# An adaptive-norm block with a gated scan and an FP4 feed-forward: loads, maxima and the last store moved to other places

## The chip, the core and the metric

The kernel runs on one NeuronCore of a Trainium2 chip. Its engines are named as in the profile: PE (matrix multiply; PEld is its weight load), DVE (vector), ACT (scalar activation), POOL (general purpose) and SP, which here only issues DMAs. Each engine works through its own instructions in program order and waits for others by semaphores. The metric is the device time of one execution in microseconds (us), as the median of several runs; one further execution was taken with the hardware profiler.

## The reference, cut to what matters

```python
mod = (silu(c) @ wmod).reshape(B, 6, 1, -1)        # sa, ca, ga, sb, cb, gb; B = 2
h = layernorm(x) * (1 + ca) + sa                    # x: 2 x 4096 x 512, fp32
xn = h / norm(h) * d**0.5 * gamma
q, kv, a = split(einsum('bnd,ed->bne', xn, W_qkva), 3)
y = scan over n of  y = sigmoid(a) * y + kv
x = x + ga * (q * y)
h = layernorm(x) * (1 + cb) + sb
gate, up = fp4_linear(h, w_gate), fp4_linear(h, w_up)   # 512 -> 1408
x = x + gb * fp4_linear(silu(gate) * up, w_down)        # 1408 -> 512
```

`fp4_linear` rounds both operands to a 4-bit grid in blocks of 16, each block scaled by its largest absolute value, before the product. ga and gb are kept at least 0.25 away from zero.

## The kernel before, in words

Every product is made from 16-bit halves: a factor is split into a high and a low part ("hl") and three of the four products are summed, 36 matmuls for one 128-row part of q, kv and a over 512 tokens. A tile of tokens is 128 rows; there are 64 (NT). A DMA transpose issued by SP brings each hl into the layout that PE needs.

*Part one* (`start()` and the loop at L766) makes norm, projection, scan and residual. A block is 512 tokens, 16 blocks in all (NBLK). A **slot** is one block and one quarter e of the 512 features, so 64 slots (NS); three more drain the pipeline. In slot s PE makes a, kv and q of that quarter (`mix`, L384) into three of six PSUM banks, which alternate between even and odd slots. One slot later ACT makes the sigmoid (`gates`, L405), DVE the scan (L411) and the product with q (L420), ACT splits y into 16-bit halves (L427), and SP transposes them; two slots later ACT joins the halves (L435) and POOL adds them to x and stores the rows to `out` (L443, L445). Beside it the norm of the tiles of the next block runs: `norm_load`, `norm_moments`, `norm_stats` (POOL, L160 and L161), `norm_center` (L166), `norm_shift` (L172), `norm_square` (ACT, L354), `norm_gain` (POOL, L359 and L361), `norm_hi` (ACT, L367), `norm_lo` (DVE, L372) and the transpose into xT (L376). The tile for which slot s issues its xT is s + 4, so the last xT of a block is issued in the slot before PE starts on it.

The projection's weights come in four groups e of three 128 x 512 parts: `load_qkva`, `gamma_qkva` (times gamma, L281, on POOL or DVE), `square_qkva` (ACT, L285), `inverse_qkva` and `gain_qkva` (POOL powers, L289 and L299; `scale_qkva` calls both), `hi_qkva` and `lo_qkva` (L310, L316) with a transpose into wqT (L324). Groups 0 to 2 are prepared in `start()`, group 3 in slots 0 and 1.

The weights of the feed-forward are prepared in the background, by a written-out plan of **units**, one step of the plan a slot: slots 6 to 16 take block maxima of the gate and up weights, slots 17 to 22 those of the down weights (`weight_max`), then `spread_max` sends the maxima of the 128 partitions through DRAM (L483, L484) and a slot later `finish_max` reduces them (L489); from then on each slot rounds one tile of weights (`quant_rows`, `quant_down`). A unit's load is issued one slot before its work. `Unit.advance` interleaves its steps with the norm's.

Near the end of part one, slot 58 (NS - 6) loads three modulation rows for part two, each spread over 128 partitions (L267), and four tiles of x from `out` (`load_x1`, L575).

*Part two* (the loop at L957) goes over the 64 tiles of tokens: `products` (gate and up, L871), `silu`, `gated`, `quant_h`, and two tiles later `down` (L918) and `finish`, which multiplies by gb and adds to `out` with an accumulating DMA of POOL (L941). `quant_x` prepares the tile two ahead.

The order on every engine is the order of the program text (`manual_schedule`). SP's DMAs count on eight semaphores in turn, so each also waits until the eighth before it has landed. The tiles "ld" are a ring of six, "hl" of four, "o" of three.

Of the kernel before, what the change touches and what calls it, by code (L numbers as in the profile page):

```python
# [17 lines left out]
P = 128  # L18
D = 512
# [24 lines left out]
def tile_adaln_block(  # L44
# [173 lines left out]
    def mod_spread(s, b):  # L218
        pm = side((P, D))
        for k in range(KC):  # L220
            T.matmul(
                pm,
                sc[:, k, b : b + 1].to_broadcast([P, P]),
                wm[s][:, k, :],
                start=k == 0,
                stop=k == KC - 1,
            )
        return pm
# [47 lines left out]
    def load_qkva(e):  # L276
        for part in (2, 1, 0):
            load_part(e, part)
# [51 lines left out]
    def norm_load(g):  # L330
        i, t = divmod(g, KC)
        if i not in xrows:
            xrows[i] = apool.tile([P, KC, D], F32, name="xr", tag="xr", bufs=4)
        xld[g] = xrows[i][:, t, :]
        b, t0 = divmod(g * P, N)
        S.dma_start(xld[g], x[b, t0 : t0 + P, :])
# [130 lines left out]
    def weight_max(wt, am, col, first):  # L467
        block_max(am, wt)
        V.tensor_scalar(am, am, 6e-12, TIE / 6.0, ALU.max, ALU.mult)
        if first:  # L470
            V.tensor_reduce(gsum[:, col : col + 1], am, AX.X, ALU.max)
        else:
            m = small.tile([P, 1], F32, name="gm", tag="gm")
            V.tensor_reduce(m, am, AX.X, ALU.max)
            V.tensor_tensor(gsum[:, col : col + 1], gsum[:, col : col + 1], m, ALU.max)
# [2 lines left out]

    peaks = []

    def spread_max():
        gall = apool.tile([P, P, 3], F32, name="gall", tag="row", bufs=1)
        G.dma_start(gmax, gsum)  # L483
        G.dma_start(gall, gmax.unsqueeze(0).to_broadcast([P, P, 3]))  # L484
        peaks.append(gall)

# [50 lines left out]
    downs = [(i, j) for i in range(KC) for j, _ in WIDE]  # L537
    for n in range(0, len(downs), 2):
        plan.append([("maxd", r) for r in downs[n : n + 2]])
    plan.append([("spread", None)])  # L540
    plan.append([("finish", None)])
    for n, r in enumerate(rows):
# [68 lines left out]
    class Unit:  # L611
# [9 lines left out]
        def advance(self, pos):  # L621
            if self.kind in ("rows", "down"):
                if pos == self.step:
                    next(self.gen, None)
                    self.step += 1
            elif pos == 3:
                if self.kind == "max":
                    i, col, _, ams = self.arg
                    weight_max(self.wt, ams[i], col, i == 0)
                elif self.kind == "maxd":  # L630
                    i, j = self.arg
                    weight_max(self.wt, am_d[i][j], 2, self.arg == (0, 0))
                elif self.kind == "spread":
                    spread_max()
                else:
                    finish_max()
                self.step = 7
# [4 lines left out]
    def start():  # L642
        a, b_, c_ = PARTS

        def load_mod_piece(s, k):
            S.dma_start(wm[s][:, k, :], wmod[k * P : (k + 1) * P, s * D : (s + 1) * D])

        load_mod(1, KC)
        norm_load(0)
        S.dma_start(gam, gamma.partition_broadcast(P))  # L650
        for k, then in enumerate((PARTS[0], PARTS[1], PARTS[2], None)):
            if then is None:
                norm_load(1)
            else:
                load_part(0, then)
            load_mod_piece(0, k)
        norm_load(2)
        norm_load(3)
        pc = mod_spread(1, 0)
        ps = mod_spread(0, 0)  # L660
        r1 = mod_rows(1)
        r0 = mod_rows(0)

        norm_moments(0)
        norm_stats(0)
        gamma_qkva(0, a, V)
        A.activation(ca[0], pc, AF.Copy, bias=1.0)
        square_qkva(0, a)
        gamma_qkva(0, b_, V)
        square_qkva(0, b_)  # L670
        inverse_qkva(0, a, a + 1)
        norm_center(0)
        gamma_qkva(0, c_, V)
        inverse_qkva(0, b_, b_ + 1)
        hi_qkva(0, a, True)
        square_qkva(0, c_)
        lo_qkva(0, a)
        inverse_qkva(0, c_, c_ + 1)
        hi_qkva(0, b_, True)
        norm_moments(1)  # L680
        norm_stats(1)
        lo_qkva(0, b_)
        A.copy(sa[0], ps)
        norm_center(1)
        hi_qkva(0, c_, True)
        norm_shift(0)
        norm_square(0)
        lo_qkva(0, c_)
        load_qkva(1)
        norm_gain(0, G)  # L690
        norm_shift(1)
        norm_square(1)
        norm_hi(0)
        norm_moments(2)
        norm_moments(3)
        norm_gain(1, G)
        norm_stats(2)
        norm_hi(1)
        norm_stats(3)
        norm_lo(0, xT)  # L700
        load_mod(2)
        norm_center(2)
        norm_shift(2)
        norm_square(2)
        norm_lo(1, xT)
        load_qkva(2)
        norm_gain(2, G)
        norm_center(3)
        norm_shift(3)
        norm_square(3)  # L710
        norm_gain(3, G)
        norm_hi(2)
        gamma_qkva(1, a, V)
        norm_lo(2, xT)
        norm_load(KC)
        norm_hi(3)
        gamma_qkva(1, b_, V)
        square_qkva(1, a)
        square_qkva(1, b_)
        norm_lo(3, xT)  # L720
        norm_load(KC + 1)
        inverse_qkva(1, b_, a + 1)
        gamma_qkva(1, c_, V)
        mod_store(*r1, tag="yh")
        square_qkva(1, c_)
        mod_store(*r0)
        hi_qkva(1, a, False)
        inverse_qkva(1, c_, c_ + 1)
        for part in PARTS:
            gamma_qkva(2, part)  # L730
        lo_qkva(1, a)
        hi_qkva(1, b_, True)
        norm_moments(KC)
        hi_qkva(1, c_, True)
        lo_qkva(1, b_)
        norm_stats(KC)
        lo_qkva(1, c_)
        norm_load(KC + 2)
        load_qkva(3)
        norm_center(KC)  # L740
        for part in PARTS:
            square_qkva(2, part)
        norm_shift(KC)
        norm_square(KC)
        norm_gain(KC, G)
        gain_qkva(0)
        norm_moments(KC + 1)
        inverse_qkva(2)
        norm_stats(KC + 1)
        for part in PARTS:  # L750
            hi_qkva(2, part, False)
            lo_qkva(2, part)
        gain_qkva(1)
        gain_qkva(2)
# [8 lines left out]
    with order:  # L763
        xT = new_xT()
        start()
        for slot in range(NS + 3):  # L766
# [19 lines left out]
                residual(*joined(*joining.pop(0)))  # L786
            if g < NT:
                norm_hi(g)
            if slot == 0:
                for part in PARTS:  # L790
                    gamma_qkva(3, part)
                    square_qkva(3, part)
            if gate is not None:
                gate = scan(*gate)
            if slot == 1:
# [9 lines left out]
                joining.append(halves(*gate))  # L805
            if slot == 1:
                for part in PARTS:
                    hi_qkva(3, part, False)
                    lo_qkva(3, part)
            if g + 2 < NT:  # L810
                norm_stats(g + 2)
            for u in units:
# [6 lines left out]
            if g + 1 < NT:  # L819
                norm_shift(g + 1)  # L820
                norm_square(g + 1)
            for u in units:
                u.advance(4)
            coming = [Unit(*c_) for c_ in coming]
# [1 line left out]
                u.advance(0)  # L826
            if g + 1 < NT:
                norm_gain(g + 1, G)
            for u in units:
                u.advance(5)  # L830
                u.advance(6)
            assert all(u.step == 7 for u in units)
            if slot == 0:
                scale_qkva(3)
            if 0 < slot < KC:
                prep_gain(slot)
            if slot + 2 in MODS:
# [3 lines left out]
            if slot == KC + 1:  # L841
                ca[1] = mod_load(1, 1, "mod_c1")
                sa[1] = mod_load(0, 1, "mod_s1")
            if slot == NS - 6:
                mods_for(0)
                gbs[0] = mod_load(5, 0, "mod_gb")
                x1s = {n: load_x1(n) for n in range(4)}
            if NS - 5 <= slot < NS - 1:
                n = slot - NS + 5
                xst[n] = stats_x(x1s[n])  # L850
# [77 lines left out]
    def finish(i, pd, u):  # L928
        b, t0 = divmod(i * P, N)
        if b not in gbs:  # L930
            t = ring.tile([P, D], F32, name="mod_gb1", tag="mod_gb1", bufs=1)
            S.dma_start(t, modd[5][b : b + 1, :].to_broadcast([P, D]))
            gbs[b] = t
        o = ring.tile([P, D], F32, name="o", tag="o", bufs=3)
        parts = 2 if i == NT - 1 else 1
        for d0 in range(0, D, D // parts):
            d = slice(d0, d0 + D // parts)
            V.scalar_tensor_tensor(  # L938
                out=o[:, d], in0=pd[:, d], scalar=u, in1=gbs[b][:, d], op0=ALU.mult, op1=ALU.mult
            )  # L940
            G.dma_start(out[b, t0 : t0 + P, d], o[:, d], accum_op=ALU.add)  # L941

    LAG, LEAD = 2, 2
    qh = {}
# [9 lines left out]
    with tc.manual_schedule(engines={V.engine, A.engine, G.engine, S.engine, T.engine}):  # L954
        h = None
        ended = []
        for i in range(NT):  # L957
# [27 lines left out]
            h = quant_h(i, work_i[2])  # L985
            step(h, 3)
        step(h, 2)
        finish(*ended.pop(0))
        step(h, 3)
        ended.append(down(NT - 2))  # L990
# [45 lines left out]
```

## Time and profile before

| | |
|---|---|
| median of 3 runs | 1947.03 us (1947.01 to 1948.91) |
| profiled execution | 1951.17 us |
| its span | 1949.0 us |
| mean granted clock of PE | 0.992 |
| PE busy | 1912.0 us, 98% |
| DVE busy | 1601.0 us, 82% |
| ACT busy | 991.2 us, 51% |
| POOL busy | 423.2 us, 22% |
| PE's first matmul | at 4.94 us |
| PE's first matmul of part two | at 572.5 us |
| PE's last matmul ends | at about 1942.3 us |

All times in views of the trace are us from the start of the span. A line of the timeline gives start, duration, engine, source line, operation, output and input, count, and in brackets how long the engine stood idle before and what released it. The releaser is inferred from the semaphores, and where several were waited for it is the last by the profile. The row of an issuing DMA (SPq, or POOL with DMA_DIRECT2D) is the time of the issue, not of the transfer. A window row gives its length, the busy time of PE, PEld, DVE, ACT and POOL, then the clock that was granted to PE (1.00 is full speed), the busy share of the DMA engines and GB/s.

### The profile page before, as it was taken

Reading aid. Unit: us, or ns where it says so; the run is one execution under the profiler, and the core shown is the slowest. Engines: PE = TensorE matmul, PEld = TensorE weight load, DVE = VectorE, ACT = ScalarE, POOL = GpSimd, SP = SyncE. Lnnn points to the kernel's source line nnn. Section 1 sums busy time; section 2 is a strip of 40 time slices with the busy share of each in tenths; the row PEclk is TensorE's granted clock in tenths of the full one; section 3 lists DMA queues with packets and bytes.
Section 4 is the critical chain, followed back from the end, with each engine's and each line's share of the span. In section 5 each row is a group of like instructions: output and inputs, shape, how many; then the busy total and the mean of one; then the engine's idle time right before and its main releaser. Section 6 shows DMA issues by size and latency. Waiting matters only on the chain.

```text
span 1949.0 us, 25684 instructions
## 1 busy us (share of the span) xinstructions
PE 1912.0 (98%) x9220; PEld 901.3 (46%) x9220; DVE 1601.0 (82%) x2669; ACT 991.2 (51%) x1705; POOL 423.2 (22%) x605
## 2 busy tenths in 40 slices
PE   7799999999999999999999999999999999999998
PEld 4344434444444444444444444444444444444443
DVE  5677889999859988888888888888888888888864
ACT  4444467777655544444444444544454454444432
POOL 4544456666530100000000000001001000000000
PEclk9899999999999999999999999999999999999999
DMA  9688689999843443533443344334434433433333
GB/s 235 145 238 199 171 169 200 202 203 200 187 103 63 78 78 63 82 74 63 73 80 67 63 79 88 63 68 88 69 63 78 79 63 64 82 73 63 68 62 51
DMA packets 483007, 206.39 MB, mean 106 GB/s; under 512 B 439558, under 2 KB 440838, under 8 KB 482880
## 3 DMA queue, kind: packets, MB, share of 16 engines
q1 hardware_dynamic: 468144, 170.98, 41.9%
q0 software_dynamic: 14736, 33.78, 10.6%
q8 instruction: 72, 1.18, 0.3%
q14 instruction: 55, 0.45, 0.1%
HBM read 62.85 MB, written 33.58 MB: 49 GB/s over the span
## 4 chain that ended last, share of the span: by engine, by line
PE 79%; issue 5%; DVE 1%; DMA 1%; POOL 0%; SPq 0%; ACT 0%; POOLq 0%; ACTq 0%; DVEq 0%
PE mm L871 44%; PE sd L918 21%; PE mm L393 14%; DMA xT<-hl 1%; POOL out_dram L941 0%; DVE ld L172 0%; DVE y L420 0%; DVE hl L372 0%; DVE ld L166 0%; SPq L575 0%; DVE xn L106 0%; DVE st L153 0%; SPq L267 0%; SPq L529 0%; DVE hl L129 0%
## 5 line engine op out<-in xcount | busy, mean ns | idle before, releaser
L871 PEld LDWEIGHTS <-x2T 128*128 128x128 f16 x4608 | 450.8, 98 | 469.4 <-issue 1.2
L393 PE MATMUL mm<-xT,wqT 128*128 128x512 f16 (+1 forms) x2412 | 511.5, 376 | 23.9 <-DMA xT<-hl 17.0
L871 PE MATMUL mm<-wuT,x2T 128*128 128x512 f16 (+1 forms) x2304 | 487.7, 361 | 1.0 <-DVE hid L891 1.0
L871 PE MATMUL mm<-wgT,x2T 128*128 128x512 f16 (+1 forms) x2304 | 487.7, 361 | 0.0
L918 PE MATMUL sd<-wdT,hT 128*128 128x512 f16 x2112 | 465.8, 379 | 0.0
L393 PEld LDWEIGHTS <-wqT 128*128 128x128 f16 x2412 | 233.5, 99 | 303.3 <-issue 37.7
L918 PEld LDWEIGHTS <-hT 128*128 128x128 f16 x2112 | 206.7, 98 | 242.6
L886 ACT ACTIVATE silu<-mm,u 128x512 f32<-128x512 f32 (+1 forms) x192 | 124.7, 650 | 285.3 <-PE mm L871 281.4
L891 DVE SCALAR_TENSOR_TENSOR hid<-mm,u,silu 128x512 f32<-128x512 f32 (+1 forms) x192 | 128.5, 673 | 140.0 <-PE mm L871 131.0
L587 POOL TENSOR_SCALAR rstd<-vs 128x1 f32<-128x1 f32 x64 | 15.2, 238 | 986.2 <-ACT sq L585 986.2
L143 ACT ACTIVATE u<-ud,rms 128x1 f32<-128x1 f32 x64 | 18.9, 295 | 278.2 <-DVE rms L139 278.2
L120 ACT ACTIVATE sle<-sl 128x512 f16<-128x512 f32 (+2 forms) x162 | 146.9, 907 | 0.0
L113 ACT ACTIVATE she<-sh 128x1408 bf16<-128x1408 bf16 (+1 forms) x128 | 128.3, 1003 | 4.0
L941 POOL DMA_DIRECT2D out_dram<-o x65 | 58.0, 898 | 275.7 <-DVE o L938 271.9
L411 DVE TENSOR_TENSOR_SCAN y<-sig,cy,mm 128x512 f32<-128x512 f32 x56 | 71.6, 1279 | 52.2 <-ACT sig L405 22.2
L427 ACT COPY yh<-y 128x1024 uint16<-128x1024 uint16 x64 | 66.9, 1046 | 79.8 <-DVE y L420 75.6
L122 DVE SCALAR_TENSOR_TENSOR xn<-hid,xn 128x1408 f32<-128x1408 f32 x64 | 103.6, 1618 | 3.7 <-ACT hid L116 3.7
L106 DVE TENSOR_TENSOR xn<-hid,inv 128x1408 f32<-128x1408 f32 x64 | 104.0, 1625 | 2.2
L125 DVE SCALAR_TENSOR_TENSOR hhl<-hid,xn 128x1408 f16<-128x1408 f32 x64 | 104.0, 1625 | 2.2
L147 DVE TENSOR_REDUCE amh<-hid 128x88 f32<-128x1408 f32 x64 | 103.7, 1620 | 2.2
L116 ACT ACTIVATE hid<-xn 128x1408 f32<-128x1408 f32 x64 | 88.2, 1378 | 30.9 <-DVE xn L106 30.9
L443 POOL TENSOR_TENSOR xr<-xr,y 128x512 f32<-128x512 f32 x64 | 81.4, 1273 | 56.4 <-ACT y L435 54.4
(113 smaller groups left out, 1913.0 us busy)
## 6 DMA issues: line engine op xcount, KB each, us to landing
xr<-in_L_attn_x_dram SPq DMA_DIRECT2D x64, 256.0 KB, 3.5
out_dram<-xr POOLq DMA_DIRECT2D x64, 256.0 KB, 4.0
ld<-out_dram SPq DMA_DIRECT2D x64, 256.0 KB, 2.9
out_dram<-o POOLq DMA_DIRECT2D x63, 256.0 KB, 4.1
ld<-in_L_ffn_w_gate_dram SPq DMA_DIRECT2D x22, 256.0 KB, 3.4
ld<-in_L_ffn_w_up_dram SPq DMA_DIRECT2D x22, 256.0 KB, 3.4
scratch<-in_L_wmod_dram SPq DMA_DIRECT2D x4, 1024.0 KB, 5.7
ld<-in_L_ffn_w_down_dram SPq DMA_DIRECT2D x16, 256.0 KB, 3.4
```

Source lines behind the costliest of these rows:

```text
L106: V.tensor_tensor(blocks(xn), blocks(src), spread(inv, nb), ALU.mult)
L113: A.activation(blocks(she), spread(sh, nb), AF.Copy, scale=WPEAK)
L116: A.activation(a, xn, AF.Abs, scale=MAGIC)
L120: A.activation(blocks(sle), spread(sl, nb), AF.Copy, scale=WPEAK)
L122: V.scalar_tensor_tensor(out=xn, in0=a, scalar=FLOOR, in1=xn, op0=ALU.max, op1=ALU.add)
L125: V.scalar_tensor_tensor(out=nq, in0=a, scalar=FLOOR, in1=xn, op0=ALU.max, op1=ALU.subtract)
L147: V.tensor_reduce(am, src.rearrange("p (b k) -> p b k", k=QB), AX.X, ALU.max, apply_absolute_value=True)
L393: T.matmul(pp[:, t : t + width], wqT[:, wp * KC + k, r * P : (r + 1) * P], xT[:, xp * KC + k, t : t + width], start=n == 0, stop=n == 3 * ...
L871: T.matmul(pp[:, : n1 - n0], x2T[:, xp * KC + k, :], wt[:, wp * KC + k, n0:n1], start=n == 0, stop=n == 3 * KC - 1,)
L886: A.activation(sl[:, :w], pairs[j][0][:, :w], AF.Silu, scale=u[:, 0:1])
L891: V.scalar_tensor_tensor(out=hid[:, n0:n1], in0=pairs[j][1][:, : n1 - n0], scalar=u[:, 1:2], in1=sl[:, : n1 - n0], op0=ALU.mult, op1=ALU.mult,
L918: T.matmul(pd, hT[:, hp * IC + k, :], wdT[:, wd_chunk(wp, k), :], start=n == 0, stop=n == 3 * IC - 1,)
```

## The change

- In `start()` the loads of the second weight group and of the first tile of block 1 go out before the first transposes; the 1 MB load of wmod (`load_mod(2)`) goes behind the second tile's xT, and the loads of the third weight group behind the fourth.
- The fourth weight group: its products with gamma (POOL) move to the end of slot 0, behind the norm's gain; its squares (ACT) from slot 0 to slot 1, behind the halves of y; scales, high and low parts (POOL, DVE) to the end of slot 1, behind the norm's shift and square.
- The maxima take three slots: `collect_max` issues the store in one, `spread_max` the load in the next, `finish_max` follows in the third. All later units move by one slot.
- At the end of part one the modulation rows are loaded in slots 36 and 38, and two tiles of x each in slots 58 and 59.
- The last tile of tokens isn't added to `out` by the DMA: DVE adds x, loaded by SP beforehand, and SP stores the sum in two halves.

```diff
+    def collect_max():
+        G.dma_start(gmax, gsum)
+
     def spread_max():
         gall = apool.tile([P, P, 3], F32, name="gall", tag="row", bufs=1)
-        G.dma_start(gmax, gsum)
         G.dma_start(gall, gmax.unsqueeze(0).to_broadcast([P, P, 3]))
...
+    plan.append([("collect", None)])
     plan.append([("spread", None)])
     plan.append([("finish", None)])
...
         norm_load(2)
         norm_load(3)
+        load_qkva(1)
+        norm_load(KC)
         pc = mod_spread(1, 0)
...
         lo_qkva(0, c_)
-        load_qkva(1)
         norm_gain(0, G)
...
         norm_lo(0, xT)
-        load_mod(2)
         norm_center(2)
         norm_shift(2)
         norm_square(2)
         norm_lo(1, xT)
-        load_qkva(2)
+        load_mod(2)
         norm_gain(2, G)
...
         norm_lo(2, xT)
-        norm_load(KC)
         norm_hi(3)
...
         norm_lo(3, xT)
+        load_qkva(2)
         norm_load(KC + 1)
...
             if g < NT:
                 norm_hi(g)
-            if slot == 0:
-                for part in PARTS:
-                    gamma_qkva(3, part)
-                    square_qkva(3, part)
...
             if slot == 1:
                 for part in PARTS:
-                    hi_qkva(3, part, False)
-                    lo_qkva(3, part)
+                    square_qkva(3, part)
...
                 norm_shift(g + 1)
                 norm_square(g + 1)
+            if slot == 1:
+                scale_qkva(3)
+                for part in PARTS:
+                    hi_qkva(3, part, False)
+                    lo_qkva(3, part)
...
             if g + 1 < NT:
                 norm_gain(g + 1, G)
+            if slot == 0:
+                for part in PARTS:
+                    gamma_qkva(3, part)
...
-            if slot == 0:
-                scale_qkva(3)
...
-            if slot == NS - 6:
+            if slot == NS // 2 + KC:
                 mods_for(0)
+            if slot == NS // 2 + KC + 2:
                 gbs[0] = mod_load(5, 0, "mod_gb")
-                x1s = {n: load_x1(n) for n in range(4)}
+            if slot in (NS - 6, NS - 5):
+                for n in range(2):
+                    n += 2 * (slot - NS + 6)
+                    x1s[n] = load_x1(n)
...
-        parts = 2 if i == NT - 1 else 1
-        for d0 in range(0, D, D // parts):
-            d = slice(d0, d0 + D // parts)
+        def scaled(d):
             V.scalar_tensor_tensor(
                 out=o[:, d], in0=pd[:, d], scalar=u, in1=gbs[b][:, d], op0=ALU.mult, op1=ALU.mult
             )
-            G.dma_start(out[b, t0 : t0 + P, d], o[:, d], accum_op=ALU.add)
+
+        if i < NT - 1:
+            scaled(slice(0, D))
+            G.dma_start(out[b, t0 : t0 + P, :], o, accum_op=ALU.add)
+            return
+        for d0 in range(0, D, D // 2):
+            d = slice(d0, d0 + D // 2)
+            scaled(d)
+            V.tensor_tensor(o[:, d], o[:, d], last_x1[:, d], ALU.add)
+            S.dma_start(out[b, t0 : t0 + P, d], o[:, d])
...
         step(h, 2)
+        last_x1 = load_x1(NT - 1)
         finish(*ended.pop(0))
```

More of the change, by code (lines that the diff above doesn't have):

```diff
@@ L632, in advance @@
                     weight_max(self.wt, am_d[i][j], 2, self.arg == (0, 0))
+                elif self.kind == "collect":
+                    collect_max()
                 elif self.kind == "spread":
```

## The prediction, made blind

> **What bounds the kernel now.** I read the waits of PE first, then PE alone in order of time, then the engines around each gap, then the granted clock in windows of 2 us. PE is busy 98% of the span, so only its idle time and the time at a lowered clock can be won. Its waits, as engine, line, what was waited for, total us, times, longest:
>
> ```profile
> PE mm L393 <- DMA xT<-hl: 17.0, 6, 5.7
> PE mm L393 <- ACT sig L405: 6.9, 2, 4.7
> PE sd L221 <- DMA scratch<-in_L_wmod_dram: 5.4, 3, 4.9
> PE mm L871 <- DVE hid L891: 1.0, 1, 1.0
> ```
>
> Nearly all of it is part one (L393). In order of time (start, duration, count, and in brackets the idle time before):
>
> ```profile
> 26.23 2.17 PE L393 MATMUL mm<-xT,wqT 128*128 128x128 f16 x36 [2.65 <-DMA xT<-hl]
> 31.88 5.54 PE L393 MATMUL mm<-xT,wqT 128*128 128x128 f16 x72 [3.48 <-DMA xT<-hl]
> ...
> 56.30 18.72 PE L393 MATMUL mm<-xT,wqT 128*128 128x512 f16 x72 [4.69 <-ACT sig L405]
> 80.75 41.58 PE L393 MATMUL mm<-xT,wqT 128*128 128x512 f16 x180 [5.72 <-DMA xT<-hl]
> ...
> 251.95 32.93 PE L393 MATMUL mm<-xT,wqT 128*128 128x512 f16 x144 [2.18 <-ACT sig L405]
> 286.90 243.36 PE L393 MATMUL mm<-xT,wqT 128*128 128x512 f16 x1119 [2.02 <-DMA xT<-hl]
> ```
>
> A slot is 36 such matmuls at 216 ns, 7.78 us. Counting them, the gaps lie inside slot 0 (26, 32), before slot 2 (56.30), slot 4 (80.75), slot 24 (251.95), slot 28 (286.90) and slot 60 (539.76, 2.38 us, also xT). Between slots 4 and 24 PE has no gap. After a gap PE also runs slowly for a while: 144 matmuls in 32.93 us instead of 31.1. The windows around slot 24 show why (the seventh figure is the clock, behind the five engines):
>
> ```profile
> 252.00:254.00 2.00, 2.00 (x8) 0.84 (x9) 0.95 (x2) 0.04 (x1) 0.00 (x0) 0.80 1.14 221
> 254.00:256.00 2.00, 2.00 (x6) 0.76 (x5) 0.00 (x0) 0.00 (x0) 0.44 (x1) 0.50 0.54 47
> 256.00:258.00 2.00, 2.00 (x10) 0.79 (x8) 0.05 (x1) 0.80 (x2) 1.84 (x4) 0.84 0.73 82
> ```
>
> 2 us x (0.20 + 0.50 + 0.16) = 1.7 us lost on top of a gap of 2.18.
>
> **A rule that would shrink the gain.** The Trainium skill ("TensorE: Matmul & The Clock Gate", section "Why this matters for your kernels") asks for no idle gaps over about 3 us between bursts, since one idle window brings the half clock. By it, gaps of 2.0 to 2.4 us cost only themselves. The rows disagree: the three gaps at slots 24, 28 and 60 are all shorter, and each is followed by the half clock (slot 28: 1.6 us lost in the windows 286 to 292; slot 60: 144 matmuls in 32.93 us, 1.8 lost). I take the rows. By the rule my sum would be 3.4 us smaller.
>
> **Maxima over three slots (slot 28).** POOL and what hung on it, in slots 23 and 24:
>
> ```profile
> 250.00 0.64 POOL L483 DMA_DIRECT2D gmax<-gsum  x1
> 255.56 0.56 POOL L484 DMA_DIRECT2D gall<-gmax  x1 [4.92 <-DMA gmax<-gsum]
> ...
> 257.12 0.72 ACT L367 ACTIVATE hl<-ld,rn 128x512 f16<-128x512 f32 x1 [5.07 <-POOL rn L361]
> ```
>
> POOL stands 4.92 us for the first DMA; behind it on POOL are L359 and L361, which ACT's L367 needs, and behind that DVE (5.00 us). The scans run 251.08, 263.34, then every 7.56: one slot of 12.3. So xT for slot 28 was issued at 281.70 and landed about 286.7, while PE was ready at 284.88. With the second DMA a slot later nothing is queued behind a wait: the first DMA (5.3 us from issue to landing) is down before POOL gets there, and the second (3.9) before DVE reads gall another slot on. Gain 2.02 + 1.6 = 3.6. The gap before slot 24 stays: xT of slot 23 was issued at 248.15, before all this, because the maxima slots take the other engines 8.35 us (scans 228.21, 236.56, 244.91) against PE's 7.78. It moves with the start. All weight work runs a slot later, at 7.56 us of DVE a slot against 7.78, and its last unit falls in slot 59, where DVE has no norm work left (it idled 7.15 us there): 0.
>
> **Loads off the end of part one (slot 60).** SP's queue before the last xT:
>
> ```profile
> 528.39 1.52 SPq L267 DMA_DIRECT2D mod<-modd  x3
> ...
> 529.96 1.92 SPq L575 DMA_DIRECT2D ld<-out_dram  x4
> 531.99 3.38 SPq L376 DMA_TRANSPOSE xT<-hl  x1
> ```
>
> Seven loads of 256 KB stand ahead of it; it takes about 7.6 us to land (539.6), against 4.9 median in slots 43 to 59. PE was ready at 537.39. Afterwards two loads stand ahead. The two that go to slot 59 are issued behind it; three go to slots 36 and 38. Issue at 531.2 (its data is ready at 531.13), landing 4.9 plus at most 1.5 for 512 KB at the 330 GB/s of these windows: 536.1 to 537.6, so the gap is 0 to 0.2. Gain 2.38 + 1.8 = 4.2. ACT's first stats_x, which waited 4.50 us for its load, then ends before the gates of slot 59 rather than with them, so nothing is late behind it. The three loads moved to slots 36 and 38 are bounded by the same landings: a block's last xT is issued 6.0 us before PE wants it (344.71 against 350.75), median landing 4.6, the longest 6.3; 256 KB in the slot before adds up to 0.8. I take 0, at worst one gap of 0.5 with its clock, 2.2.
>
> **The start (slots 0 to 4).** Freed of the 1 MB wmod load and weight loads ahead of it, xT of tile 1 need not take 7.3 us (issued 24.61, landed 31.88) but 2.8 to 4.2 (the wqT median; tile 0). The three gaps of slot 0, 6.8 us with their clock loss on top, mostly go. By itself that is worth nothing: slot 2 waits for the first sigmoid, which hangs on the side engines.
> - DVE's 4.23 us wait for tile 4's row goes, too. But the third weight group is now loaded behind all four xT. DMA is full from 20 to 40 us, the bytes are the same, so its landing is 34 to 38 us; POOL then multiplies it, 3 x 1.24, with tile 4's rstd (L160, at 38.42 now) queued behind. That starts between 37.7 and 41.7: +0.8 to -3. I take 0, for 35.
> - Fourth group: now POOL's three gamma products (50.01 to 54.17) and ACT's three squares (to 54.93) stand before ACT's square of tile 5 (54.96) and the sigmoid (55.59). Moved behind, the square follows DVE's shift at 50.9, the sigmoid starts at 51.7 and the scan at 52.4 instead of 56.29: 3.9 earlier.
> - It is partly given back in slot 1: POOL's products now run 52.6 to 56.3, ACT's squares follow the halves of y (57.4 to 59.7), then two pow on POOL (2 x 0.86), then hi and lo on DVE, 3 x 1.23, before the second scan: 64.9 instead of 67.08. 2.2 is left.
> - From there to slot 4 the loop is as before (6.05 and 6.16 us a scan), so xT of tile 7 and PE's slot 4 come 2.2 earlier; a shorter gap there (5.72 now) saves perhaps 0.3 of clock. 2.5 in all. The other engines are behind PE from slot 4 to 24, so all of it is passed on.
>
> **The last tile.** DVE adds two 256-wide sums (0.37 each, half of L281's 0.69 plus start-up) after its 0.44 products. Now the second store is issued by POOL at 1943.6 and lands 3.7 later, 1947.3. SP would issue it at 1944.0; a plain store on SP is not in the trace; nearest are SP's 256 KB loads from the same tensor (2.9, issue 0.43): 1946.9, gain 0.4. Ends: 2.0 (the tiny loads) and 4.1 (POOL's stores), so +1.3 to -0.8. The added x1 load goes out behind the transpose of tile 62, long before tile 63's: 0.
>
> **Sum.** 3.6 + 4.2 + 2.5 + 0.4 = 10.7. The profiled execution took 1951.17 (span 1949.0 and 2.2 around it), so 1940.5; it lies 4.1 above the median of 1947.03, so 1936.3 there.
>
> **Rivals.**
> 1. The start gives nothing, POOL waiting for the third group until 38 (-3 + 2.5): 1939. For: DMA is full there. Against: 1 MB now moves in the window 16 to 20, where DMA is busy only 0.6. 15%.
> 2. The last xT is still late by 0.5 to 1 behind two loads, a weight transpose and a y transpose, with its clock: 1938.8. For: slack of only 1.3. 13%.
> 3. The start gives 5 or more, the third group landing by 34 and slot 4's slow phase gone: 1933. 13%.
> 4. Slower: the DMA queues have no spare from slot 26 on (share 0.95 to 0.99), so the 768 KB put at slots 36 and 38 are never worked off, and xT comes late at all six block starts from slot 40 to 60: 6 x (1.0 + 1.7) = 16 lost against 10.7 won, 1952. It decides from a landing of 6.0 us on (4.6 now). Against it: single windows go far above 1, and 400 GB/s was moved early on against 200 here, so there is spare. 3%.
> 5. Two of the three big terms fail: 1943. 4%.
>
> The sum as it stands has 52%. The range 1931.5 to 1941.5 takes in the first three and the ends of the start. A measurement of this kernel tells about 0.2%, 3.9 us: faster by more 92%, within 5%, slower 3%.
>
> **What would show it.** No PE gap before slots 28 and 60, and no half clock there; gmax and gall DMAs about 7 us apart with no POOL wait; the last xT landing in about 5 us. A gap before slot 24 of about 2 us still. First scan near 52.4, second near 65, PE's slot 4 near 78.3. Wrong if POOL's second gamma group starts after 37, or new gaps stand at slots 40 or 60.

## The result, and the profile after

The changed kernel takes 1940.56 us (median of 7 runs, 1939.85 to 1944.22) against 1947.03 for the kernel before on the same chip (7 runs): the ratio is 0.9966 [0.9955, 0.9978], a gain of 6.6 us (4.3 to 8.8). The profiled execution took 1940.56, its span is 1938.8, so the two spans differ by 10.2 and the two medians by 6.5. That difference turns out to be the main lesson.

The waits of PE, as before (engine, line, what was waited for, total us, times, longest):

```profile
PE mm L393 <- DMA xT<-hl: 9.5, 4, 4.9
PE sd L221 <- DMA scratch<-in_L_wmod_dram: 7.1, 4, 4.9
PE mm L393 <- DMA wqT<-hl: 5.7, 1, 5.7
PE mm L393 <- ACT y L435: 2.3, 1, 2.3
```

xT falls from 17.0 us in six waits to 9.5 in four; a wait of 5.7 for a weight transpose is new. PE alone in order of time:

```profile
35.15 6.28 PE L393 MATMUL mm<-xT,wqT 128*128 128x128 f16 x72 [4.88 <-DMA xT<-hl]
54.24 5.34 PE L393 MATMUL mm<-xT,wqT 128*128 128x512 f16 x24 [1.50 <-ACT sig L405]
...
68.53 10.49 PE L393 MATMUL mm<-xT,wqT 128*128 128x512 f16 x36 [5.69 <-DMA wqT<-hl]
82.02 39.13 PE L393 MATMUL mm<-xT,wqT 128*128 128x512 f16 x180 [3.01 <-DMA xT<-hl]
...
250.93 126.17 PE L393 MATMUL mm<-xT,wqT 128*128 128x512 f16 x576 [2.33 <-ACT y L435]
377.94 186.64 PE L393 MATMUL mm<-xT,wqT 128*128 128x512 f16 x864 [0.85 <-ACT cy L414]
```

The gaps before slots 28 and 60 are gone: 576 matmuls (slots 24 to 39) and 864 (slots 40 to 63) run through, the latter at the full 216 ns each. The gap before slot 24 is still there, as said. A small one stands before slot 40. Slot 4 starts at 82.02, not at 78.3, but its gap is shorter, and a new gap of 5.69 stands one slot earlier. POOL around the maxima, the two DMAs 6.2 us apart and without a wait:

```profile
248.84 0.64 POOL L482 DMA_DIRECT2D gmax<-gsum  x1
...
255.02 0.63 POOL L486 DMA_DIRECT2D gall<-gmax  x1
```

SP's queue before the last xT:

```profile
525.08 1.04 SPq L578 DMA_DIRECT2D ld<-out_dram  x2
527.31 1.28 SPq L376 DMA_TRANSPOSE xT<-hl  x1
```

Two loads stand ahead of it, its issue takes 1.28 us instead of 3.38, and PE does not wait.

**Where the profiles' 10.2 us lie.** PE starts part two at 572.52 before and 564.42 after. On the way, after is ahead by 1.0 at slot 24 and by 3.1 at slot 28 (the 2.0 gap); the 1152 matmuls from slot 28 took 250.49 before, 1.6 above 1152 x 0.216, and this slow stretch is gone; the gap of slot 60 is worth 2.4 and its slow stretch 1.8; slot 40 costs 0.85. That is 1.0 + 2.1 + 1.6 + 2.4 + 1.8 - 0.85 = 8.1. Part two takes 1369.8 in both. From PE's end to the end of the span it is 6.72 before and 4.55 after: 2.2, by the plain stores of SP, as the DMA issues of the last 25 us show (KB each, median us to landing). All profiles of this document agree: 6.57 to 6.86 without these stores, 4.46 to 4.55 with them. After:

```profile
out_dram<-o POOLq DMA_DIRECT2D x3, 256.0 KB, 4.2
out_dram<-o SPq DMA_DIRECT2D x2, 128.0 KB, 1.7
```

Before:

```profile
out_dram<-o POOLq DMA_DIRECT2D x2, 128.0 KB, 3.3
```

### The profile page after: what moved, and what is told of

Same layout as the page of the kernel before. It is cut to its first block, busy times and chain, and to the rows that moved or that the text cites. A ratio compares the mean times of both kernels' runs of the same rounds, so it can differ in the third digit from the quotient of the medians.

```text
span 1938.8 us, 25685 instructions
## 1 busy us (share of the span) xinstructions
PE 1905.6 (98%) x9220; PEld 900.1 (46%) x9220; DVE 1603.8 (83%) x2671; ACT 993.3 (51%) x1705; POOL 419.6 (22%) x603
## 3 DMA queue, kind: packets, MB, share of 16 engines
q8 instruction: 72, 1.18, 0.2%
## 4 chain that ended last, share of the span: by engine, by line
PE 83%; DVE 2%; issue 1%; ACT 1%; DMA 0%; POOL 0%; ACTq 0%; POOLq 0%; DVEq 0%
PE mm L881 45%; PE sd L928 24%; PE mm L393 14%; DMA yt<-yh 0%; POOL xr L443 0%; DVE ld L172 0%; DVE xn L106 0%; DMA out_dram<-xr 0%; DVE xn L122 0%; POOL out_dram L445 0%; DVE y L420 0%; ACT y L435 0%; DVE hl L372 0%; DVE ld L166 0%; DVE hid L901 0%
## 5 line engine op out<-in xcount | busy, mean ns | idle before, releaser
L393 PE MATMUL mm<-xT,wqT 128*128 128x512 f16 (+1 forms) x2412 | 506.1, 373 | 20.4 <-DMA xT<-hl 9.5
L427 ACT COPY yh<-y 128x1024 uint16<-128x1024 uint16 x64 | 67.0, 1047 | 83.3 <-DVE y L420 75.2
```

What stands on the lines that cost most here:

```text
L393: T.matmul(pp[:, t : t + width], wqT[:, wp * KC + k, r * P : (r + 1) * P], xT[:, xp * KC + k, t : t + width], start=n == 0, stop=n == 3 * ...
```

## The experiments

Each ratio is to the kernel before on the same chip, and the us beside it are that ratio taken on the median of before there. Plain differences of the medians come out somewhat otherwise for the parts alone: 2.1, 3.7, 2.0, -1.0 and 3.1 us for `e1` to `e5`. Theory: the four parts are independent, slots 28 and 60 bring most, and the start brings its share through an earlier first scan. The rival: the start gives nothing, because POOL waits for the third weight group.

### The kernel before once more, and each part alone

`e0_before` is the kernel before, unchanged.

> The kernel before, unchanged, profiled once more. In the profiled executions the span fell by 10.2 us (1949.0 to 1938.8), in the medians the time fell by 6.5. Theory S (the profiled execution of before was a slow sample of its own kernel): this profile has a span near 1945, with the gaps of PE at slots 28 and 60 as before (2.0 and 2.4 us) but less lost in slots 0 to 4, where the loads decide. Theory R (the gaps are smaller in ordinary executions, and the profiler enlarges them): the span is again near 1949, and the timed median near 1947.

Measured 0.9996 [0.9988, 1.0004]; profiled span 1946.4, 2.6 less than the first profile of the very same kernel. Its trace says where:

```profile
121.00 3.60 PE L233 MATMUL sd<-scratch,sc 128*2 128x512 f32 x8
...
250.83 32.93 PE L393 MATMUL mm<-xT,wqT 128*128 128x512 f16 x144 [2.31 <-ACT y L435]
286.04 248.80 PE L393 MATMUL mm<-xT,wqT 128*128 128x512 f16 x1152 [2.28 <-ACT hl L367]
537.31 32.93 PE L393 MATMUL mm<-xT,wqT 128*128 128x512 f16 x144 [2.47 <-DMA xT<-hl]
```

The gaps before slots 28 and 60 are as large as in the first profile, but no slow stretch follows slot 28 (248.80 is 1152 x 0.216), and the start is 1.3 us earlier (the row of L233 follows slot 8; it stood at 122.26). What the first profile showed is therefore not what each run loses.

`e1_max3`: only the maxima over three slots.

```diff
+    plan.append([("collect", None)])
     plan.append([("spread", None)])
```

> Only the maxima over three slots. Theory S and the prediction: the gap before slot 28 and its half clock go, 3.6 us (1943.4 by the median). Theory R: 1.5 to 2.5 us. Rival: the later units hit something in slots 26 to 59, gain under 1 us.

Measured 0.9983 [0.9977, 0.9990], 3.3 us (2.0 to 4.5) gained. Its trace has no gap before slot 28. The interval takes in the forecast 3.6 and the upper half of theory R's 1.5 to 2.5.

`e2_endloads`: only the loads of the end of part one, as the change has them.

```diff
-            if slot == NS - 6:
+            if slot == NS // 2 + KC:
                 mods_for(0)
+            if slot == NS // 2 + KC + 2:
...
+            if slot in (NS - 6, NS - 5):
```

> Only the loads taken from the end of part one (rows in slots 36 and 38, tiles of x in 58 and 59). Prediction: the gap before slot 60 and its half clock go, 4.2 us; the changed kernel shows a new gap of 0.85 us before slot 40, so 3.3 (1943.7). Theory R: 1.5 to 2.5 us.

Measured 0.9975 [0.9965, 0.9986], 4.9 us (2.7 to 6.8). No gap before slot 60, a new one of 0.46 before slot 40.

`e3_last`: only the last tile.

```diff
-            G.dma_start(out[b, t0 : t0 + P, d], o[:, d], accum_op=ALU.add)
...
+            V.tensor_tensor(o[:, d], o[:, d], last_x1[:, d], ALU.add)
+            S.dma_start(out[b, t0 : t0 + P, d], o[:, d])
```

> Only the last tile stored plainly by SP. The prediction said 0.4 us; in the changed kernel the store landed in 1.7 us and the time from PE's end to the end of the span fell from 6.7 to 4.5 us. If that is the store alone: 2.2 us (1944.8). If it is a chance of the two profiles: about 0.4 (1946.6).

Measured 0.9992 [0.9985, 0.9998], 1.6 us (0.4 to 2.9). Its trace has the 2.2: 4.52 us from PE's end to the end of the span.

`e4_startloads`: only the loads of `start()`.

```diff
+        load_qkva(1)
+        norm_load(KC)
...
-        load_qkva(2)
+        load_mod(2)
...
         norm_lo(3, xT)
+        load_qkva(2)
```

> Only the loads of the start moved (second group and a row early, wmod behind the second xT, third group behind the fourth xT). Theory P (the start's loads cost, because POOL waits for the third group): in the changed kernel POOL's second gamma group began at 36.9 instead of 33.5 and the first scan would come 2 to 3 us later than before (56.3), so slot 4 near 83 and the time up by about 2 us. Theory Q (the loads help as meant, only the fourth group gives back): first scan at or before 56, time down by 0 to 1 us.

Measured 1.0006 [0.9997, 1.0015], a loss of 1.2 us whose interval takes in zero. Its POOL shows the rival at work:

```profile
36.29 4.08 POOL L281 TENSOR_TENSOR scratch<-scratch,gam 128x512 f32<-128x512 f32 x3 [2.47 <-DMA scratch<-in_L_attn_W_qkva_dram]
40.46 0.23 POOL L160 TENSOR_SCALAR rstd<-mv 128x1 f32<-128x1 f32 x1
```

These products stood at 33.49 before, without a wait, and L160 at 38.42. The first scan comes at 57.58, against 56.29 before. The six profiles that have the old start (before, `e0` to `e3`, `e8`) spread from 56.11 to 58.39, so POOL's wait is shown here, but not that it makes the scan later.

`e5_fourth`: only the fourth weight group.

```diff
-                    hi_qkva(3, part, False)
-                    lo_qkva(3, part)
+                    square_qkva(3, part)
...
+            if slot == 1:
+                scale_qkva(3)
```

> Only the fourth group moved. Prediction: first scan at 52.4 instead of 56.3, second at 64.9 instead of 67.1, slot 4 two us earlier, 2.2 us of time. Theory P: in the changed kernel two tiny DVE instructions (L252, L253) took 1.2 us each beside POOL's products, so 2.1 of it are lost and about 0 is left; the second scan near 67. Theory Q: the whole 2.2 or more lost, because PE's slot 3 waits for wqT.

Measured 0.9987 [0.9981, 0.9994], 2.5 us (1.2 to 3.7): the size forecast for the start, but not by its route. The second scan comes at 67.41, as theory P had it. PE alone:

```profile
67.65 10.65 PE L393 MATMUL mm<-xT,wqT 128*128 128x512 f16 x36 [5.68 <-DMA wqT<-hl]
80.93 39.02 PE L393 MATMUL mm<-xT,wqT 128*128 128x512 f16 x180 [2.63 <-DMA xT<-hl]
```

Slot 4 starts no earlier (80.93; 80.29 to 82.79 with the old start). But slots 4 to 8 take 39.02, where they took 40.5 to 41.7. The fourth group's weights now come late, so PE's long wait and the slow clock after it fall in slot 3, and slot 3 ends before slot 4's data is there anyway. The windows of after show the same (PE, PEld, DVE, ACT, POOL, then the clock):

```profile
68.00:70.00 2.00, 1.47 (x4) 0.58 (x5) 1.97 (x6) 0.19 (x1) 0.00 (x0) 0.50 0.76 173
70.00:72.00 2.00, 2.00 (x6) 0.69 (x5) 2.00 (x5) 1.05 (x1) 0.43 (x1) 0.50 0.89 204
...
82.00:84.00 2.00, 1.98 (x10) 0.92 (x11) 2.00 (x5) 1.17 (x3) 1.66 (x2) 1.00 0.60 148
84.00:86.00 2.00, 2.00 (x11) 0.94 (x10) 1.09 (x2) 0.81 (x4) 1.44 (x2) 1.00 0.78 179
```

Half clock from 68 to about 73, full clock from 82 on. In the kernel before, half clock stood from 80.75 to 86, on the path. This does not come each time: slots 4 to 8 take 39.0 to 39.1 us in `e5`, `e9`, after and `f2`, but 40.7 and 40.8 in `f1` and `f3`, whose starts are those of after and `f2`. There the gap before slot 4, 3.5 us, was followed by the half clock again.

### Parts together

`e8_oldstart`: the change with the start and the fourth group left as before, so the parts of e1, e2 and e3 together.

> Maxima, end loads and last tile as changed; start loads and fourth group as before. If the start's two edits are worth what the profile of the changed kernel shows at slot 24 (1.0 us earlier than before), this is 1 us slower than the changed kernel: ratio to before about 0.9971. If the parts add (3.3, 4.9 and 1.6 us in their own runs): 0.995, faster than the changed kernel (0.9966), and the start's edits cost some 3 us.

Measured 0.9965 [0.9952, 0.9977], 6.8 us, where the three alone sum to 9.8 (by plain medians 6.7 and 7.8). Before slot 40 its gap is 1.40, where e2 alone had 0.46.

`e9_fourth`: the change without the loads of the start.

> As the kernel before in the start's loads, all else as changed. If only the start's loads cost (theory P), this is the best of the four: 2 us under the changed kernel, ratio about 0.9955. If the fourth group costs as well, it is slower than the version that has neither.

Measured 0.9959 [0.9947, 0.9971], 8.0 us. The first scan is at 52.34, the forecast 52.4; in after, with the loads, it is at 54.22. So the loads of the start may cost the whole change some 1.4 (8.0 against 6.6; alone 1.2), but each of these intervals is wider than that.

### What holds slot 40, and what holds the second scan

SP's queue and ACT in slots 36 and 37 of after:

```profile
353.20 1.05 SPq L267 DMA_DIRECT2D mod<-modd  x2
...
354.68 1.05 ACT L427 COPY yh<-y 128x1024 uint16<-128x1024 uint16 x1 [1.08 <-DVE y L420]
...
355.39 1.59 SPq L376 DMA_TRANSPOSE xT<-hl  x1
357.08 3.95 SPq L429 DMA_TRANSPOSE yt<-yh  x1
...
363.94 1.05 ACT L427 COPY yh<-y 128x1024 uint16<-128x1024 uint16 x1 [2.58 <-DMA yt<-yh]
```

Two row loads of 256 KB go out together. The transpose of y behind them takes 3.95 us to issue, and there is one buffer yh, so ACT's next halves wait 2.58 us for it. At the same place before:

```profile
361.58 2.34 SPq L429 DMA_TRANSPOSE yt<-yh  x1
```

In after the two L427 lie 9.26 us apart, where a slot is 7.78. The third row in slot 38 then stands right ahead of an xT, and PE waits 0.85 at slot 40.

`f1_rows`: after, with the three rows one each in slots 35, 39 and 43.

```diff
-            if slot == NS // 2 + KC:
-                mods_for(0)
-            if slot == NS // 2 + KC + 2:
+            if slot == NS // 2 + KC - 1:
+                mods[0] = (mod_load(4, 0, "mod_c0"),)
+            if slot == NS // 2 + KC + 3:
+                mods[0] += (mod_load(3, 0, "mod_s0"),)
+            if slot == NS // 2 + KC + 7:
```

> The changed kernel with its three modulation rows loaded one each in slots 35, 39 and 43 instead of two in 36 and one in 38. Theory Y (the gap before slot 40 comes from the two loads of slot 36 holding up the transpose of y, so that ACT waits 2.58 us for the only yh buffer, and from the load of slot 38 right ahead of the block's last xT): the gap of 0.85 us (1.4 and 2.0 in two versions) is gone and ACT's wait for yh under 0.5 us; about 1 us of time. Theory Z (DMA has no spare from slot 26 on, so 768 KB delay some block's xT wherever they go): a gap stays before slot 40 or comes before slot 36 or 44.

Measured 0.9959 [0.9946, 0.9973], 1940.19. PE runs through from slot 24:

```profile
251.76 312.65 PE L393 MATMUL mm<-xT,wqT 128*128 128x512 f16 x1440 [2.32 <-ACT y L435]
```

All 40 slots without a gap, as in `f3` and `f6`, whose rows stand in the same slots; all five profiles with rows in 36 and 38 have one (0.46 to 1.98 us). ACT's halves come every 7.77 us and no longer wait for yh. So the place of the row loads was the cause. Which of theory Y's two reasons does it, the buffer or the load right ahead of xT, is not shown, since `f1` takes away both. The time gained is below what these intervals tell apart.

Now the second scan. DVE and POOL after the first scan in after:

```profile
54.22 1.22 DVE L411 TENSOR_TENSOR_SCAN y<-sig,mm 128x512 f32<-128x512 f32 x1 [1.43 <-ACT sig L405]
54.55 3.72 POOL L281 TENSOR_TENSOR scratch<-scratch,gam 128x512 f32<-128x512 f32 x3
55.86 1.21 DVE L252 TENSOR_SCALAR mag<-mag 128x8 f32<-128x8 f32 x1
57.11 1.18 DVE L253 SCALAR_TENSOR_TENSOR gq<-gq,mag 128x8 f32<-128x8 f32 x1
...
59.20 0.73 DVE L420 SCALAR_TENSOR_TENSOR y<-mm,gq,y 128x512 f32<-128x512 f32 x1
59.97 1.05 ACT L427 COPY yh<-y 128x1024 uint16<-128x1024 uint16 x1 [4.22 <-DVE y L420]
60.92 0.63 ACT L285 ACTIVATE sq<-scratch 128x512 bf16<-128x512 f32 x1
```

Two tiny operations on 128 x 8 numbers take 1.21 and 1.18 us; before, they ran when POOL's products were over:

```profile
57.92 0.16 DVE L252 TENSOR_SCALAR mag<-mag 128x8 f32<-128x8 f32 x1
58.12 0.17 DVE L253 SCALAR_TENSOR_TENSOR gq<-gq,mag 128x8 f32<-128x8 f32 x1
```

The products (1.24 each) now run beside them, and each of the two ends as a product ends: at 57.07 and 58.29, the second and third product at about 57.03 and 58.27. The Trainium skill ("SBUF — State Buffer", section "Who interferes with whom") names a mechanism that fits: DVE and POOL share one pair of ports as an exclusive lock, and a DVE operation that needs it, such as one with two inputs from SBUF (L253) or a tensor-scalar form in a two-port mode (L252 can be one; the trace doesn't say), waits for the whole POOL instruction. The operation ahead of these two (L251), with the same products running but its input in PSUM, took its usual 0.17. What hangs on them follows in the fence: y, its halves, the squares behind these on ACT, and so the second scan at 68.28.

`f2_floor`: e9 with these operations (and `prep_gain(0)` behind them) in slot 0, ahead of POOL's products.

```diff
                 norm_shift(g + 1)
+                if slot == 0:
+                    signed_floor(gq, cols, atile([P, KC, B], F32, "mag"))
+                    prep_gain(0)
                 norm_square(g + 1)
```

> The version with the start's loads as before (all else as changed), with the five tiny DVE instructions for gq (L251 to L253 and the two gains) in slot 0, between shift and square, ahead of POOL's products with gamma. Theory C (a DVE instruction on SBUF data waits while POOL runs a product: L252 and L253 took 1.2 us each instead of 0.17): second scan about 64.3 instead of 66.4, slot 4 two us earlier, 1.5 to 2 us of time. Rival: POOL's products only move the wait to another DVE instruction, or PE's slot 3 waits for wqT anyway: under 0.5 us.

Measured 0.9956 [0.9943, 0.9968], 1939.38. DVE in its trace:

```profile
52.29 0.16 DVE L252 TENSOR_SCALAR mag<-mag 128x8 f32<-128x8 f32 x1
52.49 0.17 DVE L253 SCALAR_TENSOR_TENSOR gq<-gq,mag 128x8 f32<-128x8 f32 x1
...
57.12 1.66 DVE L166 SCALAR_TENSOR_TENSOR ld<-xr,mv,ca 128x512 f32<-128x512 f32 x1
...
64.68 1.22 DVE L411 TENSOR_TENSOR_SCAN y<-sig,mm 128x512 f32<-128x512 f32 x1
```

They are short again. The rival holds in part, as L166 now takes 1.66 us beside the products (0.72 in after), but from the first scan to the second it is 10.96 us instead of 14.06 in after (14.04 in e9, 14.06 in e5). Its span is 1935.2, 3.0 below that of e9, of which 2.1 are there at slot 24; the medians' intervals cannot tell the two apart.

`f3_both`: e9 with the edits of f1 and f2.

> Both: rows one each in slots 35, 39, 43 and the gq instructions in slot 0, start's loads as before. If the two add: 3 us under the version with the start's loads as before (ratio 0.9959), about 0.9945, and 4 us under the changed kernel.

Measured 0.9946 [0.9934, 0.9958], 1936.71: 10.5 us less than before, as forecast (0.9945). On the same chip f1 took 1940.19 and f2 1939.38. With `f6`, which equals it, it is the fastest version measured.

`f6_q2early`: f3 with the loads of the start moved up as in the change, but the third group left behind the second xT, and the 1 MB load of wmod behind the fourth xT. Against `f3`:

```diff
+        load_qkva(1)
+        norm_load(KC)
...
-        load_qkva(1)
...
-        load_mod(2)
...
-        norm_load(KC)
...
+        load_mod(2)
```

> The last one with the start's loads moved as in the change, except that the third weight group stays behind the second xT and the 1 MB of wmod goes behind the fourth. Theory P (what cost in the start's loads is POOL's wait for the third group): POOL's second gamma group starts at 33.5 again, the first scan at or before 52.3, time equal to the last one or up to 1 us less. Rival (the loads cost in another way, DMA being full): 1 us slower.

Measured 0.9947 [0.9935, 0.9960], 1937.14, equal to f3. POOL's products for the third group start at 33.95 without a wait and the first scan is at 52.33. So POOL's wait comes from the place of the third group, which `f6` exchanges with wmod's, and moving the others up gains nothing on the path: PE's waits in slot 0 end before the first sigmoid does. That this place is also what the start's loads cost in time fits these runs, but the cost is about as small as the spread among profiles. The time at which PE has ended slot 8 (the first row of L233 behind it) shows both:

| start | profiles | PE ends slot 8 at |
|---|---|---|
| as before | before, e0 to e3, e8 | 121.0 to 124.4, mean 122.3 |
| loads moved | e4 | 123.0 |
| fourth group moved | e5, e9 | 119.9, 119.4 |
| both, as in the change | after, f1 | 121.1, 121.9 |
| fourth group moved, gq in slot 0 | f2, f3 | 117.2, 118.0 |
| the same, loads moved but the third group left | f6 | 118.4 |

## Why the prediction was right, and where its sum was not

Faster, inside the range but 0.9 us from its end, 4.3 us above the point: the sum was 10.7, the medians give 6.5.

- **The step that failed is the last one of the sum: taking all that one profile shows off a median.** In the two profiles 10.2 of 10.7 came, and that is partly luck: the start gave 1.0 of its 2.5 and slot 40 cost 0.85, and the last tile gave 1.8 more than its 0.4. The profile of before lay 4.1 above its kernel's median, and this had been read as an offset that both kernels share. There is no such offset: after has 1940.56 both as profiled time and as median, and in the 13 profiles other than the first the profiled time lies between 2.1 below and 2.5 above the median, on average 0.2 below. So the excess belonged to this execution. The second profile of the same kernel (e0, on another chip) is 2.6 shorter, mainly by 1.3 at the start and 1.7 of clock after slot 28, less some longer gaps. Of these only the clock was unusual in the first profile: its 122.26 at the end of slot 8 is the mean of the six with this start. The rest of the 4.1 was not pinned down. As an estimate, each loss at its mean over the profiles that can have it gives 0.8 (start), 2.0 + 0.3 (slot 28 and its clock), 2.6 + 1.1 (slot 60), -0.85 (slot 40) and 2.2 (last tile): about 8, inside the measured 4.3 to 8.8.
- **Slot 28: the mechanism is right, its clock term not.** Forecast 2.02 + 1.6; e1 measured 3.3 (2.0 to 4.5). POOL no longer waits and PE has no gap. The 1.6 of half clock was there in 1 of the 6 profiles that have this gap (before, not e0, e2, e3, e4, e5).
- **Slot 60: right.** Forecast 4.2; 4.9 (2.7 to 6.8) in e2, 4.2 in the profiles. The half clock followed this gap in 4 of 6 profiles, so that counting it in full was luck in part.
- **Rows at slots 36 and 38: taken as 0, "at worst one gap of 0.5 with its clock"; 0.85 in after, 1.40 and 1.98 in e8 and e9, without half clock.** A new gap at slot 40 was one of the prediction's own signs of being wrong, and it came. The bound looked at xT alone. What was queued behind the rows was also the transpose of y, and behind it ACT, by the single buffer.
- **The start's loads: taken as 0, measured +1.2 (-0.6 to 2.9).** The interval takes in the 0. Rival 1 named the mechanism, POOL's wait (2.5 to 2.8 us in e4, after and f1), and its end of the range: L160 at 41.03 in after, near the late end of 37.7 to 41.7. With the old loads L160 stands at 38.3 to 40.5, so less is lost than the 3 us of that rival.
- **The fourth group: 2.2 forecast, 2.5 measured, by another way.** The first scan came as worked out when the loads of the start were not moved (52.34 in e9, 53.35 in e5, for 52.4). The second was to follow 12.5 us later and followed 14.06 later, by the stretched DVE operations, which had been left at their 0.17. What gained in e5 was mostly the clock, moved off slot 4 into slot 3, for which 0.3 had been put down; that the size agrees is luck.
- **The last tile: right in sign, too small.** Forecast 0.4; 1.6 (0.4 to 2.9) in e3, 2.2 in the profiles. The store's landing was taken as 2.9 from SP's 256 KB loads; it is 1.7 for 128 KB.
- **The skill's clock rule.** The Trainium skill ("TensorE: Matmul & The Clock Gate", section "Why this matters for your kernels") speaks of gaps over about 3 us. The runs stand between it and the certain loss that was put down: from slot 24 to the end of part one, gaps of 2.02 to 2.91 us brought the half clock in 18 of 23 cases, gaps of 0.46 to 1.98 in none of 8. Among the 23, length does not decide: 2.02 brought it at slot 28, 2.28 and 2.67 there did not. By the rule the sum would have been 7.3, nearer the measured 6.5, though the slots 24 and 60 speak against it.

**Still open.** The five parts alone sum to 11.1, with some 3.5 either way (9.9 by plain medians); the whole gives 6.6 (4.3 to 8.8). The larger gap at slot 40 and the third group may explain part; the rest may be the intervals, or parts that don't add. What decides whether a gap of 2 to 3 us brings the half clock is not shown. Two buffers for yh were not tried.

## What to carry to other kernels

Before gains read in one profile are taken off a median, profile the same kernel again: a loss that only one of two shows counts by its frequency, and a time is held against its spread over several profiles of the same code (3.4 us at the end of slot 8 here), not against one. When loads are moved, list everything queued behind them at the new place, other transposes and single buffers too, and not only the transfer that one cares for. When work of POOL is moved, look at which small DVE operations on the path now run beside it.

## What the runs showed of the hardware

- DVE operations of 0.16 to 0.17 us took 1.2 while POOL multiplied two 128 x 512 fp32 tiles (1.24 each); ahead of these products they are short again (f2). The trace of before already showed it: L172 took 1.66 us at 50.17, beside such products, and 0.75 at 64.90, without them. The prediction used the short duration where the products left (its shift at 50.9 is 50.17 plus 0.75), and overlooked the long one where they went.
- From slot 24 to the end of part one the half clock followed 18 of 23 PE gaps of 2.02 to 2.91 us (13 of 14 at slot 24, 5 of 9 at slots 28 and 60) and none of 8 up to 1.98, each time with 1.6 to 1.8 us lost. Where PE has a second wait soon after, the slow stretch is free (slot 3 in e5 and after), unless that wait brings the half clock again (f1, f3).
- A plain SP store of 128 KB landed in 1.7 us, POOL's accumulating store of the same size in 3.3.
